# Two-layer transformer kernel: the second scores and the mixing of blocks 2 and 3 made in pairs of head groups, with block 3's queries held aside

## The chip, the core and the metric

The kernel runs on one core of a Trainium2 chip. A core has five engines that run side by side, each through its own stream of instructions, and that wait for one another through semaphores: TensorE (PE in the profile; its weight loads are PEld), VectorE (DVE), ScalarE (ACT), GpSimd (POOL) and SyncE (SP), which here only issues transfers (DMAs). SBUF is the working memory of 128 partitions, PSUM the small memory that PE writes its results to, in eight banks of 128 partitions by 512 float32 values. The metric is the time of one execution on the device in microseconds (us), as the median of several runs.

## The reference

Four layers in a row, each on the normalized input and added to it. The input x is 4 sequences of 512 tokens with 256 features.

```python
x = x + L0_attn(layernorm(x))   # 16 heads of 16, causal, over the 512 tokens of a sequence
x = x + L0_ffn(layernorm(x))    # 8 experts, the best 2 per token AND per output feature
x = x + L1_attn(layernorm(x))   # 16 query heads of 128, 4 key heads; attends over the 4 sequences
x = x + L1_ffn(layernorm(x))    # gated, 2048 inner units, weights unpacked from 4 bits

# L0_attn, the part that the change touches
qkv = einsum('bsd,od->bso', x, w_project)            # q, k, v: [b, 16, 512, 16]
att = einsum('bhqd,bhkd->bhqk', q, k) / sqrt(16)
att = softmax(where(causal, -1e9, att))
out = einsum('bhqk,bhkd->bhqd', att, v)
return einsum('bsd,od->bso', out, w_out)
```

## The kernel before

**Blocks, sequences, head groups.** The 512 positions of a sequence are four blocks j of 128. Layer 0's attention works on the queries of one block j, one sequence s and one or more head groups g (four heads each) at a time, a *batch*. Block 0 takes 4 head groups in a batch, block 1 takes 2, blocks 2 and 3 take 1, so there are 4 + 8 + 16 + 16 = 44 batches, in the order of j, then s, then g. Block j's queries meet the keys of blocks 0 to j: 384 keys for block 2, 512 for block 3. `qk` holds, per head group, four slots with the keys of the four blocks and two more (4 and 5) with queries; block j's queries go to slot 4 + j % 2, so block 2 takes over block 0's slot and block 3 takes over block 1's.

**The softmax in two passes.** The first scores (`greatest`, L631) put the queries on the partitions; `mask` (L644) adds a large negative number to the masked part and DVE takes the maximum of each row (L650, four reductions per batch, one for each head of a group). `shift` (L660, L663) transposes the maxima on PE and subtracts them on DVE from the rows of the queries that are kept for it, so that the second scores come out less the maximum. The second scores (`powers`, L679) put the keys on the partitions: for each chunk c of 128 keys and each head one matmul with 128 query columns. ACT takes the exponent (L688), POOL sets the masked part to 0 (L698). `mixed` (L715) multiplies by the values, which carry a column of ones for the softmax's sum, and ACT copies the result (L723). `divided` transposes it (L733), divides on DVE (L740, L741), transposes again (L750), and after the block's last sequence makes the output product (L762) and adds it to the residual (L772). Then `hidden_pieces` normalizes the block for the feed-forward part.

**Buffers.** PSUM has five banks for scores (`ps_sc`, used in turn by four first and four second scores), one for the transposed maxima and the mixing (`ps_mm`), and two for everything else (`ps_dn`).

**The order of the work.** For PE, DVE and POOL the order is that of the program. It is written out by a loop over the batches n. Step n emits: first scores of batch n+1, shift of n, mask and maxima of n+1; a *fill*; mixing of n-1; second scores of n; another fill. A fill opens a *slot*: it hands out a budget of estimated PE and DVE time, and takes pieces from a list of streams, in the order of the list, as long as budget is left and a piece's conditions hold (`need(engine, cost, gap, cond)`; the gap is the number of slots since the stream's last piece). The streams are the preparation of later blocks (`prepare`, `projections`), the divisions, and the feed-forward part of layer 0: `logit_pieces` and `result_pieces` (L226, the *products*, estimated at 1.85 of PE each; 128 in all, eight for each of 16 groups of 128 tokens, four of a block), `weight_pieces` (the choice of the best two, on DVE) and `addition_pieces`. What is left of the feed-forward part when layer 0's attention is done is spread over layer 1's attention, whose loop over p stands at p = 10 until the last addition.

**Preparation of a block.** `project` makes 128 rows of keys or queries for a block (L529), ACT copies them to `stage` (L533, one buffer), and eight DMAs bring the stage's keys and queries to `qk` (L539, SP's queue). Layer 1's weights for q, k, v (`wqkv`, L916) are loaded into memory that layer 0 leaves.

## Time and profile before

| | |
|---|---|
| median of 3 runs | 1183.99 us (1183.14 to 1185.19) |
| the profiled execution | 1185.96 us, its span 1184.2 us |
| PE busy | 1153.4 us, 97% of the span |
| DVE busy | 807.9 us, 68% |
| ACT busy | 485.2 us, 41% |
| block 2's batches | 138 to 263 us |
| block 3's batches | 263 to 392 us |
| second scores (L679) | 1280 records, 54.1 us |
| mixing (L715) | 1280 records, 46.2 us |
| granted PE clock | 0.995 |

The span runs from the first to the last instruction that the profile shows; the execution's own time has a little around it. Each float32 matmul is two records. Busy times are unions, so records that overlap count once. A line of the timeline has the start, the length, the engine, the line in the kernel, the operation, what it writes and reads, the shape (rows x columns of the array that are used, then the moving operand) and the number of merged records; in brackets the idle time of the engine before it and what ended that. A line of the table by stage has the length of the stretch and each engine's busy time in it with its instructions in parentheses.

### The profile page before, as it was taken

The page shows a single profiled execution, that of the slowest core. Times are in us where ns is not written, and L with a number is a line of the kernel's source. Part 1 is how long each engine was busy: PE and PEld are TensorE (multiplying, and loading weights), DVE is VectorE, ACT ScalarE, POOL GpSimd, SP SyncE. Part 2 cuts the span into 40 slices and gives each one's busy share as a digit, 9 for nine tenths or more (in the row PEclk, how much of TensorE's full clock was granted, in tenths as well). Part 3 has the DMA queues.
Part 4 walks back from the last instruction along what each step waited for, and adds up shares of the span by engine and source line. Part 5 has one row for each costly group of instructions (what it writes and reads, how often), then busy time and mean ns, then how long its engine had stood idle before and what let it go on. Part 6 is the DMA issues. An engine that isn't in the chain of part 4 may idle for free.

```text
span 1184.2 us, 18603 instructions
## 1 busy us (share of the span) xinstructions
PE 1153.4 (97%) x7178; PEld 666.0 (56%) x7178; DVE 807.9 (68%) x1783; ACT 485.2 (41%) x1099; POOL 106.4 (9%) x152
## 2 busy tenths in 40 slices
PE   7999999999999899999999999999999999999998
PEld 3666555555555445555555556566644465475487
DVE  5676779889889777368646783888599844725710
ACT  1434545555466444445344542455244322303300
POOL 7322112112111000000000000000000000000000
PEclk9999999999999999999999999999999999999999
DMA  7230010000000310000000001021010000000000
GB/s 216 66 79 2 16 22 1 2 1 1 2 1 2 117 62 1 1 1 1 1 1 1 1 7 31 18 65 26 18 52 4 0 1 18 0 1 18 1 12 24
DMA packets 21240, 26.46 MB, mean 22 GB/s; under 512 B 5128, under 2 KB 14600, under 8 KB 21152
## 3 DMA queue, kind: packets, MB, share of 16 engines
q1 hardware_dynamic: 20480, 24.10, 7.4%
q10 hardware_dynamic: 672, 1.18, 0.4%
q8 instruction: 56, 0.92, 0.3%
q14 instruction: 32, 0.26, 0.1%
HBM read 18.97 MB, written 2.10 MB: 18 GB/s over the span
## 4 chain that ended last, share of the span: by engine, by line
PE 82%; DVE 11%; ACT 2%; issue 2%; POOL 1%; DMA 1%; SPq 0%; ACTq 0%; DVEq 0%; POOLq 0%
PE qk_ps L967 11%; PE o L1058 10%; PE y L1214 9%; PE g L895 9%; PE u L895 9%; PE lg_ps L226 8%; PE eo L226 8%; PE s L631 4%; PE s L679 3%; DVE mx L650 3%; PE av L715 2%; PE v_ps L949 2%; PE qk_ps L529 2%; PE a L1038 1%; PE s L980 1%
## 5 line engine op out<-in xcount | busy, mean ns | idle before, releaser
L967 PE MATMUL qk_ps<-xT,wqkv 128*128 128x512 f32 x320 | 148.6, 598 | 0.3 <-ACT qT L971 0.3
L226 PE MATMUL lg_ps<-rw,xT 128*128 128x512 f32 x256 | 123.6, 607 | 3.9 <-ACT xT L934 1.6
L226 PE MATMUL eo<-ew,xT 128*128 128x512 f32 x256 | 122.4, 601 | 3.2 <-ACT part L315 1.0
L1058 PE MATMUL o<-wpj,oT 128*128 128x256 f32 x512 | 119.8, 382 | 0.0
L1214 PE MATMUL y<-wd,it 128*128 128x256 f32 x512 | 111.8, 379 | 0.0
L1058 PEld LDWEIGHTS o<-wpj,oT 128*128 128x128 f32 x512 | 95.7, 190 | 27.7 <-issue 15.1
L1214 PEld LDWEIGHTS y<-wd,it 128*128 128x128 f32 x512 | 97.0, 190 | 15.0 <-issue 2.2
L650 DVE TENSOR_REDUCE mx<-s 128x1 f32<-128x384 f32 (+3 forms) x176 | 100.5, 633 | 1.4 <-PE s L644 1.4
L967 PEld LDWEIGHTS qk_ps<-xT,wqkv 128*128 128x128 f32 x320 | 59.4, 190 | 68.7 <-issue 59.6
L688 ACT ACTIVATE pt<-s 128x512 f32<-128x512 f32 (+1 forms) x176 | 83.7, 560 | 23.4 <-PE s L679 23.4
L895 PE MATMUL g<-xT,wgu 128*128 128x512 f32 x192 | 90.4, 593 | 0.0
L895 PE MATMUL u<-xT,wgu 128*128 128x512 f32 x192 | 90.2, 592 | 0.0
L315 ACT ACTIVATE part<-eo,c 128x256 f32<-128x256 f32 x128 | 53.8, 472 | 86.5 <-PE eo L226 85.0
L698 POOL TENSOR_SCALAR_AFFINE_SELECT pt<-pt 128x256 f32<-128x256 f32 (+2 forms) x88 | 60.7, 696 | 266.5 <-ACT pt L688 265.8
L1192 ACT ACTIVATE th<-sq 128x512 f32<-128x512 f32 x64 | 40.3, 630 | 87.8 <-DVE sq L1191 87.8
L226 PEld LDWEIGHTS eo<-ew,xT 128*128 128x128 f32 x256 | 46.4, 191 | 49.0 <-issue 37.4
L226 PEld LDWEIGHTS lg_ps<-rw,xT 128*128 128x128 f32 x256 | 46.3, 191 | 49.2 <-issue 36.8
L214 DVE TENSOR_TENSOR xres<-xres,y 128x256 f32<-128x256 f32 x16 | 6.7, 421 | 92.2 <-PE y L1214 92.2
L177 POOL TENSOR_TENSOR ln_rs<-rs_v,minus_half 128x4 f32<-128x4 f32 x16 | 18.0, 1124 | 553.2 <-DVE rs_v L176 455.6
L631 PE MATMUL s<-qk 32*128 32x128 f32 (+3 forms) x512 | 62.2, 465 | 1.2 <-ACT pt L688 0.9
L1193 DVE SCALAR_TENSOR_TENSOR th<-th,g 128x512 f32<-128x512 f32 x63 | 43.2, 686 | 29.2 <-ACT th L1192 29.2
L289 ACT COPY lg<-lg_ps 128x512 f32<-128x512 f32 x64 | 37.6, 587 | 62.1 <-PE lg_ps L226 61.9
(233 smaller groups left out, 1763.2 us busy)
## 6 DMA issues: line engine op xcount, KB each, us to landing
qk<-stage SPq DMA_DIRECT2D x56, 64.0 KB, 2.4
wqkv<-in_w_qkv SPq DMA_DIRECT2D x8, 320.0 KB, 7.4
rw<-in_router_w SPq DMA_DIRECT2D x8, 256.0 KB, 7.5
ew<-in_expert_w SPq DMA_DIRECT2D x8, 256.0 KB, 4.6
wpj<-in_w_proj SPq DMA_DIRECT2D x1, 2048.0 KB
out<-xres SPq DMA_DIRECT2D x4, 512.0 KB, 2.6
xres<-in_x SPq DMA_DIRECT2D x3, 512.0 KB, 9.1
dq_wgu<-in_gate_w SPq DMA_DIRECT2D x8, 128.0 KB, 2.4
```

The costliest lines, as they stand in the source:

```text
L226: nc.tensor.matmul(ps, lhsT=xT[:, hc, (g % 4) * P : (g % 4 + 1) * P], rhs=w[:, hc, 2 * pair : 2 * pair + 2, :].rearrange("p e o -> p (e o) ...
L315: nc.scalar.mul(part[:, e % 4], ps[:, i], c[:, e : e + 1])
L631: nc.tensor.matmul(tiles[h][:, b * nk : (b + 1) * nk].rearrange("p (c k) -> p c k", k=P), lhsT=queries(j, g)[r, s], rhs=qk[r, g, : j + 1, ...
L650: nc.vector.tensor_reduce(maxes[n % 2][:, h, gs[0] : gs[0] + nb], ps[:, : nb * nk].rearrange("p (b k) -> p b k", b=nb), AX.X, ALU.max,)
L688: nc.scalar.activation(pt[:, i, : nb * nk], tiles[2 * pair + i][:, : nb * nk], AF.Exp, scale=0.25)
L698: nc.gpsimd.affine_select(out=last, in_=last, compare_op=ALU.is_ge, fill=0.0, base=0, pattern=pattern, channel_multiplier=-1,)
L895: nc.tensor.matmul(ps, lhsT=wgu[:, w, half, jj, par * P : (par + 1) * P], rhs=xT[:, half, :], start=half == 0, stop=half == 1,)
L967: nc.tensor.matmul(ps, lhsT=wqkv[:, hc, kv, h, :], rhs=xT[:, hc, :], start=hc == 0, stop=hc == 1,)
L1058: nc.tensor.matmul(ys[t // 2][:, t % 2], lhsT=state["o"][:, h, t * P : (t + 1) * P], rhs=wpj[:, HPK * kv + h, :], start=kv == 0 and h == 0 ...
L1192: nc.scalar.activation(th, sq, AF.Tanh, scale=0.7978845608028654)
L1193: nc.vector.scalar_tensor_tensor(th, th, 1.0, gp, ALU.add, ALU.mult)
L1214: nc.tensor.matmul(ps, lhsT=it[:, c // 2, c % 2, t * P : (t + 1) * P], rhs=wd[:, c // 2, c % 2, :], start=c == 0, stop=c == 2 * NJ - 1,)
```

## The change

Batches 0 to 11 (blocks 0 and 1) stay. From batch 12 on, the batches of blocks 2 and 3 alternate: for each s and g first block 2's, then block 3's. The first scores, masks, maxima and shifts are still made per batch. The second scores and the mixing are made per *pair*:

- `pair_powers(m, 0)` takes the keys of blocks 0 and 1 against the queries of blocks 2 and 3 together (256 columns in a matmul); `pair_powers(m, 1)` takes the keys of block 3 (against block 3's queries alone) and of block 2 (against both). The second half's exponents go to a buffer `lasts`, in the memory of the projection weights `wp`, which are not needed by then; one select on POOL per two heads masks both blocks' last chunks.
- `pair_mixed(m)` adds up all four key blocks for both blocks' queries in one group of matmuls, and ACT copies the two halves.
- The loop has one step more (45). Even steps from 14 on emit `pair_powers(m, 1)` with no mixing before it, odd steps from 15 on emit `pair_mixed(m - 1)` and `pair_powers(m, 0)`.
- Block 3 has to be prepared before step 12. Its preparation starts at step 5 in place of 7. Its queries go to a stage of their own for both halves and are placed into slot 5 in two parts, s = 0, 1 after 8 batches and s = 2, 3 after 12, when block 1 no longer needs them (`place_queries`, 16 DMAs each); its keys go straight to their slot (16 DMAs).
- Blocks 2 and 3 are divided one after the other for each s (`both_divided`), and their output products, now a stream of its own (`output_0`), both come after the last pair. The normalization for layer 1's first block is made from step 40 on.
- The fills of block 3's steps get PE budgets of 1.8 and 2.2 in place of 1.6 and 2.0.

```diff
+            if j == 3:
+                nc.scalar.copy(stage[:, half] if i else stage, ps)
+                if not i:
+                    for r in range(8):
+                        h = 32 * (r % 4)
+                        nc.sync.dma_start(out=qk[h + 4 : h + 20, 2 * half + r // 4, j]...,
+                            in_=stage[16 * r : 16 * r + 16])
+                return
...
+        def place_queries(stage, s):
+            for r in range(16):
+                h, half = 32 * (r % 4), r // 8
+                nc.sync.dma_start(
+                    out=qk[h + 4 : h + 20, r // 4, 5, s : s + 2].rearrange("p s q -> p (s q)"),
+                    in_=stage[16 * (r % 8) : 16 * (r % 8) + 16, half, s * P : (s + 2) * P],
+                )
...
+            if j == 3:
+                qs = a1.tile([P, 2, 512], F32, tag="stage", name="stage3")
+                for half in range(2):
+                    yield need("PE", 1.75, 2)
+                    project(j, xT, half, qs, 1)
+                for half in range(2):
+                    yield need("PE", 1.75, 1, cond=lambda: blanked >= 10)
+                    ks = a1.tile([P, 512], F32, tag="keys", name=f"keys3_{half}")
+                    project(j, xT, half, ks, 0)
+                for s in (0, 2):
+                    yield need("PE", 0.0, 0, cond=lambda: done >= 8 + 2 * s)
+                    place_queries(qs, s)
+                return
...
+        FIRST = 12
+        batches[FIRST:] = [
+            (j, s, range(g, g + 1)) for s in range(NS) for g in range(4) for j in (2, 3)
+        ]
...
+        def pair_powers(m, second):
+            _, s, gs = batches[FIRST + 2 * m]
+            g = gs[0]
+            tiles = [ps_sc.tile([P, 512], F32, tag="sc", name=f"p{m}_{second}_{h}") for h in range(4)]
+            to = 0
+            for c in (3, 2) if second else (0, 1):
+                q = qk[:, g, 5 if c == 3 else 4 : 6, s, :]
+                at, to = to, to + q.shape[1] * P
+                for h in range(4):
+                    r = slice(32 * h, 32 * h + 32)
+                    nc.tensor.matmul(
+                        tiles[h][:, at:to].rearrange("p (c k) -> p c k", k=P),
+                        lhsT=qk[r, g, c, s, :], rhs=q[r], start=True, stop=True,
+                    )
...
+        def pair_mixed(m):
...
+            for c in range(4):
+                of, nq = (0, 256, P, 0)[c], 1 if c == 3 else 2
+                for r in range(4):
+                    at = c * per_block + (s * NH0 + 4 * g + r) * 17
+                    pt = powers_of[m, c // 2][r // 2][:, r % 2, of : of + nq * P]
+                    nc.tensor.matmul(
+                        av[32 * r : 32 * r + 32, 2 - nq : 2], lhsT=va[:, at : at + 32],
+                        rhs=pt.rearrange("p (b k) -> p b k", k=P), start=c == 0, stop=c == 3,
+                    )
...
-        for n in range(NBT):
+        for n in range(NBT + 1):
...
-            if n in (1, 7):
+            if n in (1, 5):
...
+            if n == NBT - 4:
+                streams.insert(
+                    0, Stream(norm_pieces(0, b1, b2, normed_first, cond=lambda: (3, 1) in added))
+                )
...
-                if n:
+                if 0 < n <= FIRST:
                     mixed(n - 1)
-                powers(n)
+                elif n > FIRST + 1 and not second:
+                    pair_mixed(m - 1)
+                if n < FIRST:
+                    powers(n)
+                elif n > FIRST:
+                    pair_powers(m, second)
...
-        mixed(NBT - 1)
-        streams.insert(0, Stream(norm_pieces(0, b1, b2, normed_first)))
-        last = Stream(divided(*batches[NBT - 1][:2]))
-        streams.insert(0, last)
-        while last.next is not None:
+        behind_powers = False
+        fill(PE=2.0, DVE=2.6)
+        pair_mixed(15)
+        streams.insert(0, Stream(both_divided(NS - 1)))
+        while not {4 * j + t for j in (2, 3) for t in (0, 2)} <= resolved or not normed_first:
             fill(PE=2.0, DVE=2.6)
```

## The prediction, made before the changed kernel ran

> **What bounds the kernel now.** I read the page's busy shares first, then the chain that ended last, then the table by stage for the two stretches in which blocks 2 and 3 run (138 to 263 us and 263 to 392 us, read off the transposes of the maxima at L660).
>
> ```profile
> span 1184.2 us, 18603 instructions
> PE 1153.4 (97%) x7178; PEld 666.0 (56%) x7178; DVE 807.9 (68%) x1783; ACT 485.2 (41%) x1099; POOL 106.4 (9%) x152
> ...
> PE 82%; DVE 11%; ACT 2%; issue 2%; POOL 1%; DMA 1%; SPq 0%; ACTq 0%; DVEq 0%; POOLq 0%
> ```
> ```profile
> 138.00:263.00 125.00, 120.77 (x1145) 64.58 (x1146) 102.99 (x265) 66.30 (x194) 22.06 (x34) 0.96 0.06 10
> 263.00:392.00 129.00, 125.33 (x1398) 68.92 (x1396) 112.54 (x261) 71.65 (x185) 22.05 (x33) 1.00 0.01 2
> ```
>
> The first number after the stretch is its length, then PE, PE's loads, DVE, ACT and POOL. PE is the bound everywhere, but here DVE is busy 82% and 87% of the time, so it is the second bound, and PE's busy time contains waits: a group of matmuls that stops half way is still shown as busy. So I measure each group of matmuls by its shortest form and call the rest a wait.
>
> **Second scores, the heart of the change: worth nothing.** Per pair of batches the old code issues 3 + 4 chunks of four matmuls with 128 columns (56 records, two to a matmul, in two groups). The new one issues two chunks of 256 columns, then one of 128 and one of 256: 32 records. The columns that stream are 7 x 128 = 896 in both. What is a column worth in wide and in narrow matmuls? The first scores show it, with 512 columns for four heads in three widths:
>
> ```profile
> 39.39 1.17 PE L631 MATMUL s<-qk 32*128 32x128 f32 x32
> ...
> 58.78 1.15 PE L631 MATMUL s<-qk 32*128 32x256 f32 x16
> ...
> 310.78 1.14 PE L631 MATMUL s<-qk 32*128 32x512 f32 x8
> ```
>
> 1.17, 1.15 and 1.14 us: halving the instructions gives 0.02 us. The Trainium skill speaks for the change here ("TensorE: Matmul & The Clock Gate", LDWEIGHTS): a weight load lasts its columns divided by 1.2 in ns, however few rows it has, and by its section on packing small matmuls it overlaps a running matmul only in another row group. Per row group the pair drops from 7 to 4 loads of two records, so the rule would give up to 3 x 2 x 107 ns = 0.64 us a pair, 10 us over 16 pairs. This trace's loads last 187 ns (L679), longer than the rule's, and are hidden all the same. I take the row: 16 x 0.02 = 0.3 us, called 0. Bounds: 0 to -10.
>
> **Mixing: -2.2 us.** From start to the next group's start the mixing of block 2 (24 records) takes 0.79 us at its shortest, of block 3 (32 records) 1.01: 0.22 for each chunk of 128 columns and 0.13 once per group. One group of 896 columns: 7 x 0.22 + 0.13 = 1.67 against 1.80, so 0.13 to 0.14 a pair, 16 pairs: -2.2. With one group instead of two, the wait for the only buffer of the `mm` pool (av behind L663's subtraction, 0.16 in the batch shown next) also comes half as often: waits at L715 sum to about 3 us in these stretches, a third of it saved, -1. The ACT exponents keep their columns; POOL's selects go from four to two of double width, hidden (POOL is busy 17%).
>
> **The moved cover: +6 us.** The second scores use five PSUM buffers together with the first scores of the next batch, so their fourth head waits until DVE has read the third maximum of that next batch (L650). PE issues in order: the projection, product or first score behind such a matmul waits with it, and ACT's exponents after it. Two batches show what hides this:
>
> ```profile
> 188.09 0.39 PE L644 MATMUL s<-later,ident_h 128*128 128x128 bf16 x4
> 188.41 1.98 PE L226 MATMUL eo<-ew,xT 128*128 128x512 f32 x4
> 188.49 1.95 DVE L650 TENSOR_REDUCE mx<-s 128x1 f32<-128x384 f32 x4
> 190.33 0.86 PE L715 MATMUL av<-pt,va 128*32 128x128 f32 x24
> 191.12 0.95 PE L679 MATMUL s<-qk 32*128 32x128 f32 x24
> ...
> 337.12 0.39 PE L644 MATMUL s<-later,ident_h 128*128 128x128 bf16 x4
> 337.53 2.48 DVE L650 TENSOR_REDUCE mx<-s 128x1 f32<-128x512 f32 x4
> 337.67 1.08 PE L715 MATMUL av<-pt,va 128*32 128x128 f32 x32 [0.16 <-DVE qk L663]
> 338.68 1.94 PE L679 MATMUL s<-qk 32*128 32x128 f32 x32
> ```
>
> In the first, a product of the feed-forward part (1.9 us) and the mixing (0.8) lie between mask and second scores, which run in 0.95. In the second the planner had no product, the mixing alone was the cover, and they took 1.94 instead of 1.17: 0.77 us lost. After the change the mixing stands ahead of every other second-score group only: in the steps that mask block 2's batch (odd n) the cover grows to 1.67, in those that mask block 3's (even n), whose maxima are the longer ones, it is gone. From the first mask matmul, the third maximum of a block 3 batch ends after 2.29 us when DVE is on time and up to 3.60 when it is late. With one product and no mixing the second scores start at 2.09 us, and their fourth head is due 0.11 later. Taking the mixing's 1.01 us out of the 16 block 3 batches: six with a product and DVE on time lose at most 0.09 each; six with DVE late lose 0.25, 0.59, 1.17, 0.94, 1.40 and 0; four with less than a product lose 1.86, 1.63, 1.64, 1.64. Sum 11.6, against 3.3 by the same rule today: +8.3. The odd steps save block 2's 2.3 us of such waits nearly whole: -2. Net +6. Bounds: 0 (DVE, which gains time while PE waits, is never late) to +12 (products run short more often).
>
> **Block 3's projection: -3 us.** It now runs before step 12, and its queries are copied into one buffer for both halves instead of a `stage` buffer that must be emptied by eight DMAs between the halves. Today:
>
> ```profile
> 153.30 1.11 ACT L533 COPY stage<-qk_ps 128x512 f32<-128x512 f32 x2
> 153.97 1.99 PE L762 MATMUL o<-wo,aT 128*128 128x256 f32 x8 [2.25 <-ACT stage L533]
> ```
>
> Late copies leave no PSUM buffer and PE waits; with 1.03 and 0.62 us at the projections of 138 and 148 us that is 3.9 us. I take -3, since the second half of the keys still waits for eight DMAs (2.4 us to landing, a fill slot of about 4 us between them); bounds -4 to 0. Placing costs 48 DMAs where there were 16. They stand in SP's queue, where nothing follows until the next layer's weights at 402 us; the second placing waits for the last batch of block 1 and is needed only when block 3's s = 2 starts, some 16 steps later. Cost 0; without that cover one landing, 2.4 us.
>
> **The end of the layer: +4.5 us.** Today block 2 is finished at 289 us and its tokens feed the products from 309 us on; four products of token group 8 run between 380 and 411 us. Now blocks 2 and 3 finish together, so until then only 64 products (groups 0 to 7) exist; some 60 had run by the same point today. Behind the end stand twice as many divisions and output products (4.6 us of PE work, moved and not added), two or three fill slots more, and one step more in the loop (45 for 44). Then the weights of layer 1 wait, as today, for the last output product:
>
> ```profile
> 400.35 1.99 PE L762 MATMUL o<-wo,aT 128*128 128x256 f32 x8 [0.93 <-ACT part L315]
> 402.38 6.01 SPq L916 DMA_DIRECT2D wqkv<-in_w_qkv  x10
> 408.97 1.07 ACT L934 COPY xT<-xT_ps 128x512 f32<-128x512 f32 x2 [0.18 <-DMA wqkv<-in_w_qkv]
> ```
>
> From 400.35 to the value products at 411.43 PE has 11.1 us, filled with three products of 1.81, one output product of 2.0 and 1.2 of transposes: 2.5 idle. With none or one of the three left, and one product less to wait behind, the idle part is 4.3 to 6.1: +2 to +3.5, say +2.7. For one or two missing products in the last steps, at the 0.8 that such a step loses, and the longer tail +1.8. The products themselves are not lost, layer 1 spreads what is left. Block 3's tokens still wait for group 7. Bounds 0 to +15, the upper end if the products come so late that layer 1's step 10, which waits for the last addition (740.5 us today, just in time), has to stand still.
>
> **The sum.** 0 - 2.2 - 1 + 6 - 3 + 4.5 = +4.3 us. The profiled execution took 1185.96 us (its span 1184.2 and 1.8 around it), so 1190.3 in its terms; it stands 1.97 above the median of the runs, 1183.99. Predicted: 1188.3 us.
>
> **Rivals.** (a) As summed, +2.4 to +12: 0.44. (b) DVE is not late and the cover isn't missed: the +6 becomes 0 and the end costs 2, which gives -4.2, 1180; for it speaks that the batches with a product and DVE on time lose only 0.09. It decides from the point where the third maximum is read within 2.2 us of the mask. Against it speaks DVE's 87%. 0.22. (c) The weight loads do limit the second scores: -10 and the rest as summed, 1178; the three widths speak against it: 0.05. (d) It ends within 2.4 us, gains and losses cancel, 1184: 0.17. (e) The late tokens hold layer 1 at its step 10: +15 in place of +4.5, 1199; against it, the planner shares what is left over nine steps: 0.12.
>
> **How the numbers follow.** 0.2%, 2.4 us, is about what a measurement of this kernel can tell from no change. Faster is (b) and (c), 0.27; same is (d), 0.17; slower is (a) and (e), 0.56. The likeliest case, (a), alone spans 1186.4 to 1196. The range takes in (b), (d), (a) and most of (e): 1178 to 1202.
>
> **What would show it.** Right: about 16 groups of second scores a layer with their span near 1.15 and 16 near 0.94 when they don't wait; mixing groups of some 1.7 us, 16 of them; second scores after a product alone that are stretched by DVE's maxima, hardly any after the mixing; no wait on the stage copy; fewer products between the last output product and the value products. Wrong: unstretched second scores of 896 columns a pair that take well under 1.9 us, even steps without stretch, or product supply that lasts through the end.

## The result

The changed kernel takes 1224.01 us, the median of four runs (1221.63 to 1227.1), against 1184.06 us before in the same session: a ratio of 1.0337, 95% interval 1.032 to 1.0353. It is 40 us slower. The prediction was 1188.3 us with a range of 1178 to 1202; the sign was right, the size off by a factor of about nine.

The page of the changed kernel: the span, the busy times, the granted PE clock in 40 slices (before it was 9 in every slice), and the shares of the chain that ended last.

```profile
span 1223.6 us, 16999 instructions
...
PE 1177.6 (96%) x6410; PEld 666.3 (54%) x6410; DVE 813.4 (66%) x1783; ACT 482.8 (39%) x1099; POOL 93.7 (8%) x120
...
PEclk9999889999889898999999999999999999999999
...
PE 78%; DVE 16%; ACT 2%; issue 1%; POOL 1%; DMA 1%; SPq 0%; DVEq 0%; ACTq 0%; POOLq 0%
```

PE has 24 us more of busy time although it executes 768 records fewer, and its share of the chain fell from 82% to 78% while DVE's rose from 11% to 16%. The clock row is new: it has dips in slices 5 to 16 (122 to 490 us). The mean granted clock is 0.978 where it was 0.995.

Where the time went is read from the table by stage, with stretches that begin and end at the same instruction in both kernels (steps at the transposes of the maxima, L660 before and L700 after; layer 1's groups at the transposes of their scores on DVE). First before: step 11; steps 12 to 42; from step 43 to the first scores of layer 1; the first group of layer 1.

```profile
128.82:137.88 9.06, 9.06 (x91) 4.83 (x88) 7.85 (x15) 4.61 (x10) 0.98 (x3) 1.00 0.01 2
137.88:380.51 242.63, 235.41 (x2428) 127.92 (x2427) 207.19 (x508) 131.33 (x362) 41.63 (x63) 0.98 0.03 6
380.51:438.62 58.11, 50.93 (x252) 24.47 (x249) 44.00 (x124) 29.78 (x81) 4.98 (x6) 1.00 0.28 91
438.62:466.82 28.20, 27.67 (x137) 13.99 (x138) 21.70 (x46) 12.52 (x25) 1.01 (x1) 1.00 0.00 1
```

The same four stretches after; the columns are the length, then PE, PE's loads, DVE, ACT and POOL with instructions in parentheses, then the granted clock, the DMA share and GB/s.

```profile
126.94:143.95 17.01, 14.27 (x100) 7.15 (x96) 12.16 (x18) 5.38 (x11) 1.89 (x2) 0.92 0.14 34
143.95:403.10 259.15, 245.82 (x1631) 118.95 (x1630) 216.34 (x513) 129.16 (x359) 29.30 (x32) 0.93 0.01 2
403.10:465.20 62.10, 56.25 (x275) 30.17 (x274) 28.18 (x84) 26.11 (x65) 3.29 (x4) 0.97 0.26 85
465.20:504.05 38.85, 32.20 (x139) 16.80 (x140) 30.29 (x76) 13.52 (x36) 1.77 (x1) 0.87 0.00 0
```

Four places are longer: step 11 by 7.9 us (clock 0.92), steps 12 to 42 by 16.5 (clock 0.93), the end of the layer by 4.0, the first group of layer 1 by 10.7 (clock 0.87). Steps 4 to 10 are 1.9 us shorter, the rest of layer 1 is 2.0 longer. The experiments, described below, are read by the same stretches. Each has its ratio to the kernel before in its own session, whose median lay between 1184.06 and 1185.56 us, so single differences to 1224.01 can be off by some 1.5 us.

| us | before | after | e2 | e7 | e8 | e10 | e11 | e4 | e6 |
|---|---|---|---|---|---|---|---|---|---|
| steps 4 to 10 | 60.4 | 58.5 | 59.0 | 58.4 | 58.6 | 58.8 | 58.4 | 60.3 | 60.7 |
| step 11 | 9.1 | 17.0 | 17.6 | 17.5 | 11.5 | 17.4 | 11.5 | 9.1 | 9.1 |
| steps 12 to 42 | 242.6 | 259.2 | 238.9 | 239.4 | 257.8 | 261.9 | 239.6 | 240.2 | 240.5 |
| step 43 to layer 1's first scores | 58.1 | 62.1 | 62.0 | 64.2 | 62.1 | 62.1 | 62.0 | 61.7 | 56.3 |
| layer 1, first group | 28.2 | 38.9 | 38.5 | 39.1 | 38.8 | 18.8 | 18.8 | 31.9 | 28.2 |
| groups 2 to 9 | 216.5 | 216.8 | 216.8 | 216.8 | 216.9 | 225.8 | 225.8 | 220.5 | 216.5 |
| groups 10 to 16 | 149.4 | 151.0 | 151.0 | 151.0 | 151.0 | 152.5 | 152.6 | 152.6 | 149.4 |
| time at half clock, before the kernel's end | 10.2 | 54.6 | 23.9 | 37.5 | 47.8 | 54.6 | 13.7 | 17.1 | 6.8 |

The last row is the sum of the stretches in which the trace's clock record shows 0.5; each is 3.41 us or a multiple of it. A PE that streams all the time loses half of such a stretch, so the 44 us more after the change can hold at most 22 of the 40 us.

Two steps of the changed kernel in a row, step 35, in which the second scores run freely (odd: block 2's mask at 335.12), and step 36 (even: block 3's mask at 344.35), in the timeline.

```profile
335.12 0.39 PE L684 MATMUL s<-later,ident_h 128*128 128x128 bf16 x4
...
335.34 1.94 PE L227 MATMUL eo<-ew,xT 128*128 128x512 f32 x4
...
337.20 1.07 PE L788 MATMUL av<-pt,va 128*32 128x256 f32 x16
...
338.09 0.83 PE L788 MATMUL av<-lasts,va 128*32 128x256 f32 x16
...
338.86 1.15 PE L755 MATMUL p<-qk 32*128 32x256 f32 x16
...
341.12 0.42 ACT L407 ACTIVATE spare<-owing 128x256 bf16<-128x256 f32 x1 [1.37 <-DVE owing L417]
...
341.53 2.04 ACT L766 ACTIVATE pt<-p 128x512 f32<-128x512 f32 x4
341.85 2.41 PE L671 MATMUL s<-qk 32*128 32x512 f32 x8
...
344.35 0.39 PE L684 MATMUL s<-later,ident_h 128*128 128x128 bf16 x4
...
344.67 0.48 PE L755 MATMUL p<-qk 32*128 32x128 f32 x2
344.76 2.47 DVE L690 TENSOR_REDUCE mx<-s 128x1 f32<-128x512 f32 x4
...
345.49 2.84 PE L755 MATMUL p<-qk 32*128 32x128 f32 x14 [0.34 <-DVE mx L690]
...
348.26 3.78 PE L227 MATMUL lg_ps<-rw,xT 128*128 128x512 f32 x4
```

In the first step a product (1.94) and the pair's mixing (1.07 + 0.83) lie between mask and second scores, which run in 1.15 us. Their exponents (L766) begin only at 341.53: ACT works in order, and ahead of them it has an operation of the feed-forward part (L407) that waits 1.37 us for DVE. So block 3's first scores (L671), which need the buffers that the exponents free, take 2.41 us where 1.14 is enough. In the second step there is neither a product nor a mixing. The second scores begin 0.3 us after the mask, stop after two records for a score buffer that DVE's maxima (344.76, 2.47 us long) still hold, and the whole group takes from 344.67 to 348.26, 3.6 us, where 0.9 is enough. Then the product behind it takes 3.78 us in place of the usual 1.9: the clock fell to 0.5 from 346.1 us on.

Summed over the stretch, each group from its start to the start of the next, the differences to before are (us):

| group | before | after | difference |
|---|---|---|---|
| products (49 of 1.89, 52 of 2.06) | 92.8 | 107.1 | +14.4 |
| block 3's first scores (16 of 1.41, 15 of 2.20) | 22.5 | 33.1 | +10.6 |
| second scores | 39.3 | 46.2 | +6.8 |
| masks, with the wait behind them | 9.4 | 13.8 | +4.4 |
| block 2's first scores (14 of 1.29, 15 of 1.02) | 18.1 | 15.3 | -2.8 |
| mixing | 28.9 | 26.5 | -2.4 |
| block 3's projection | 7.0 | 0 | -7.0 |
| output products | 7.6 | 3.8 | -3.9 |
| other groups | 17.1 | 13.4 | -3.6 |
| steps 12 to 42 | 242.6 | 259.2 | +16.5 |

Of the products' 14.4 us, 5.7 are three products more, and 8.8 their longer time, nearly all of it in stretches at half clock. The second scores of even steps take 1.90 us in the mean against 0.87 when nothing holds them, those of odd steps 1.18 against 1.08; that is 17 us of stretch where the kernel before had 8.7, of which 2.3 were the stage wait behind one group. So the stretch rose by some 10 us. Most of it, 13 us, lies in six even steps (30, 32, 34, 36, 38 and 42) whose first fill has no product.

Block 3's first scores do not stand behind those stretched groups. They stand in the odd steps, behind second scores that run nearly freely, and wait for their exponents. In steps 15, 25, 27 and 41 no product lies between the two, and they take 6.3, 2.9, 3.7 and 3.0 us. In steps 15, 17, 27, 31, 35 and 39 the exponents begin 2.0 to 4.0 us after the start of the second scores, with a feed-forward operation directly ahead of them on ACT, where six other odd steps have 1.2.

### The profile page after: what moved, and what is told of

Read it like the earlier page. It is cut to its first block, busy times and chain, and to the rows that moved or that the text cites. A ratio compares the mean times of both kernels' runs of the same rounds, so it can differ in the third digit from the quotient of the medians.

```text
span 1223.6 us, 16999 instructions
## 1 busy us (share of the span) xinstructions
PE 1177.6 (96%) x6410; PEld 666.3 (54%) x6410; DVE 813.4 (66%) x1783; ACT 482.8 (39%) x1099; POOL 93.7 (8%) x120
## 3 DMA queue, kind: packets, MB, share of 16 engines
q10 hardware_dynamic: 672, 1.18, 0.4%
## 4 chain that ended last, share of the span: by engine, by line
PE 78%; DVE 16%; ACT 2%; issue 1%; POOL 1%; DMA 1%; SPq 0%; DVEq 0%; ACTq 0%; POOLq 0%
PE qk_ps L1088 10%; PE y L1335 9%; PE o L1179 9%; PE g L1016 8%; PE u L1016 8%; PE lg_ps L227 8%; PE eo L227 7%; PE s L671 4%; DVE mx L690 3%; PE p L755 2%; PE v_ps L1070 2%; PE qk_ps L531 2%; PE av L788 1%; PE a L1159 1%; PE s L1101 1%
## 5 line engine op out<-in xcount | busy, mean ns | idle before, releaser
L227 PE MATMUL lg_ps<-rw,xT 128*128 128x512 f32 x256 | 131.0, 638 | 1.0 <-ACT xT L1055 0.7
L227 PE MATMUL eo<-ew,xT 128*128 128x512 f32 x256 | 124.9, 612 | 2.1 <-ACT part L316 0.8
L1179 PEld LDWEIGHTS o<-wpj,oT 128*128 128x128 f32 x512 | 95.8, 190 | 28.2 <-issue 15.6
L227 PEld LDWEIGHTS lg_ps<-rw,xT 128*128 128x128 f32 x256 | 49.3, 202 | 52.4 <-issue 46.1
L671 PE MATMUL s<-qk 32*128 32x128 f32 (+3 forms) x512 | 67.5, 481 | 6.3 <-ACT pt L766 3.5
L1016 PEld LDWEIGHTS u<-xT,wgu 128*128 128x128 f32 x192 | 36.5, 190 | 45.9 <-issue 44.5
L1016 PEld LDWEIGHTS g<-xT,wgu 128*128 128x128 f32 x192 | 36.2, 190 | 45.1 <-issue 41.3
```

The costliest lines, as they stand in the source:

```text
L227: nc.tensor.matmul(ps, lhsT=xT[:, hc, (g % 4) * P : (g % 4 + 1) * P], rhs=w[:, hc, 2 * pair : 2 * pair + 2, :].rearrange("p e o -> p (e o) ...
L671: nc.tensor.matmul(tiles[h][:, b * nk : (b + 1) * nk].rearrange("p (c k) -> p c k", k=P), lhsT=queries(j, g)[r, s], rhs=qk[r, g, : j + 1, ...
L1016: nc.tensor.matmul(ps, lhsT=wgu[:, w, half, jj, par * P : (par + 1) * P], rhs=xT[:, half, :], start=half == 0, stop=half == 1,)
L1179: nc.tensor.matmul(ys[t // 2][:, t % 2], lhsT=state["o"][:, h, t * P : (t + 1) * P], rhs=wpj[:, HPK * kv + h, :], start=kv == 0 and h == 0 ...
```

## The experiments

The steps of the prediction that could have failed so badly were the cover moved out of the even steps, the placing, and the late tokens. The first theory was the missing cover; its rivals were the order of the batches itself, SP's queue, the late tokens, and later the vector engine's work and the clock. The larger PE budgets in block 3's steps stay in every run made from the changed kernel; they were not tested alone.

**e1: the order and the placing alone.** The batches alternate as in the change, block 3 is prepared in the same way and the tokens come late, but second scores and mixing are per batch, as before.

```diff
-                elif n > FIRST + 1 and not second:
-                    pair_mixed(m - 1)
-                elif n > FIRST:
-                    pair_powers(m, second)
+                if n:
+                    mixed(n - 1)
+                powers(n)
```

> The changed kernel with the second scores and the mixing made per batch again, 128 columns at a time, a mixing in every step; what stays of the change is the alternating order, the early preparation of block 3 with its queries held aside, and the late finish of blocks 2 and 3. Theory A, the pairing itself costs the time, since every even step has lost its mixing as a cover and PE's clock drops after such waits: some 16 us of the stretch of blocks 2 and 3 come back, about 1206 us, granted clock above 0.99. Theory B, order and late tokens cost the time: no less than 1218 us.

1217.48 us, ratio 1.0278 (1.0259 to 1.0296). Most of the loss is there without any pair of second scores: step 11 is 17.0 us, the first group of layer 1 39.1, and steps 12 to 42 still take 256.3. Here the mixing stands in every step, so that the stretch is exposed in another way, in the timeline:

```profile
350.51 1.17 PE L719 MATMUL s<-qk 32*128 32x128 f32 x32
351.50 1.02 PE L671 MATMUL s<-qk 32*128 32x512 f32 x2
354.06 2.81 PE L671 MATMUL s<-qk 32*128 32x512 f32 x6 [1.54 <-ACT pt L728]
```

Here a step's second fill has no product, the first scores (L671) come directly behind the second scores and wait for the buffers that ACT's exponents (L728) still read; then the clock falls (0.5 from 355.3 us on). So neither the pair form nor a missing mixing is needed for a loss in this stretch. Why e1's stretch is 17 us longer than that of e2, which has the same order, is known in part: block 3's first scores take 2.37 us in e1 and 1.72 in e2, 9.8 us in all. In step 15 they take 5.8 against 2.7. There ACT has a feed-forward operation (L383), which waits 1.90 us for DVE, ahead of the exponents in e1, as in the changed kernel (2.25 us), and behind them in e2 and e7. The rest is open.

**e2: pairs of second scores, mixing in both steps.** The changed kernel, with each block's mixing in a step of its own.

```diff
-                elif n > FIRST + 1 and not second:
-                    pair_mixed(m - 1)
+                elif n > FIRST + 2:
+                    block_mixed(m - 1, second)
```

> The changed kernel with its wide second scores, but the mixing split by query block: block 2's in the odd steps, block 3's in the even ones, ahead of the second half's scores (the fourth buffer for exponents is the stage that is free by then). Theory A, the missing cover: the groups of second scores with 128 and 256 columns come down from a mean of 1.94 us to about 1.2, the granted clock rises above 0.99, about 1206 us. Theory B: within 4 us of the changed kernel's 1224.

1207.19 us, ratio 1.0192 (1.016 to 1.0223): 17 us are back by the medians, 19.4 by the spans, all of it in steps 12 to 42, which fall to 238.9, below the 242.6 of before. The second scores of even steps fall from 1.90 to 1.20 us in the mean, block 3's first scores from 2.20 to 1.72, and the half-clock time from 54.6 to 23.9 us.

**e3: block 3's keys on ACT's queue.** SP's queue held all 32 placing transfers ahead of the keys' 16, though the program emits the keys' first: its order is not that of the program. In the timeline of the changed kernel:

```profile
117.26 20.65 SPq L592 DMA_DIRECT2D qk<-stage  x32
...
133.81 1.88 PE L531 MATMUL qk_ps<-xT,wp 128*128 128x512 f32 x4
...
138.02 8.29 SPq L540 DMA_DIRECT2D qk<-keys  x10
...
140.07 3.94 PE L671 MATMUL s<-qk 32*128 32x512 f32 x8 [2.67 <-DMA qk<-keys]
```

The last key product is done at 135.7; the keys' transfers start at 138.02, when SP has issued the last placing (20.65 us for 32, 0.65 each), and the first scores of block 3 wait 2.67 us for the first of them and then run in pieces, 3.94 us for 1.14. The edit gives the keys another queue.

```diff
-                        nc.sync.dma_start(
+                        nc.scalar.dma_start(
                             out=qk[h + 4 : h + 20, 2 * half + r // 4, j].rearrange(
```

> The changed kernel with the 16 transfers of block 3's keys issued from ACT's queue instead of SP's, where they stand behind all 32 placing transfers, the last 16 of which wait for block 1's last batch. Theory: step 11 to 12 takes 17.0 us in the changed kernel against 9.1 before, 6 of them for the keys; they come back, about 1218 us, and the wait of PE for the keys (2.7 us at 137 us) is gone. Rival, the placing itself or the drain costs it: within 2 us of 1224.

1223.51 us, ratio 1.0325 (1.031 to 1.0341): nothing gained. The wait went over to ACT, as the timeline shows:

```profile
135.56 5.51 ACTq L540 DMA_DIRECT2D qk<-keys  x8
...
141.81 3.78 PE L227 MATMUL lg_ps<-rw,xT 128*128 128x512 f32 x4 [5.67 <-ACT lg L290]
```

Eight transfers hold ACT for 5.51 us, 0.69 each, and PE waits 5.67 us for the copy behind them. So this run didn't tell the theories apart; e8 does.

**e4: the kernel before with late tokens.** Block 2's tokens are handed to the feed-forward part only with block 3's.

```diff
+            if j == 2:
+                return
+            if j == 3:
+                streams.insert(fold_at, Stream(hidden_pieces(2)))
+                fold_at += 1
             streams.insert(fold_at if j else 0, Stream(hidden_pieces(j)))
```

> The kernel before, with one thing of the change: block 2's tokens are handed to the feed-forward part only when block 3's are, at the end of layer 0's attention. If the late tokens cost what the end of layer 0 and the first head group of layer 1 lost in the changed kernel (4 and 10.6 us), about 1198 us; if the planner makes up for them in layer 1, within 3 us of 1184, as I had predicted no more than 2 for them.

1197.53 us, ratio 1.0108 (1.0091 to 1.0125), 12 us slower than before (1185.56 in that session) by this one edit. The end of the layer takes 3.6 us more, the first group of layer 1 3.7, groups 2 to 9 4.0 and groups 10 to 16 3.2; steps 12 to 42 get 2.4 shorter. The prediction had looked for the price at the end of the layer only and set 4.5.

**e5: the changed kernel, with idle matmuls in the empty even fills.** Two matmuls that write to a spare buffer stand where an even step's first fill had given PE nothing.

```diff
+            if n > FIRST and second and left["PE"] == given:
+                ps = ps_dn.tile([P, 512], F32, tag="dn", name=f"warm_{n}")
+                for i in range(2):
+                    nc.tensor.matmul(ps, lhsT=ident, rhs=wo..., start=not i, stop=i == 1)
```

> The changed kernel with two extra matmuls of 512 columns (1.8 us, result not used) in those even steps whose first fill gave PE nothing, so that PE works while it would wait for DVE's maxima of 2.5 us; nothing is left out. If half of the loss in blocks 2 and 3 is the clock that drops after such waits (54 us at half speed in the changed kernel, 11 before), the granted clock rises towards 0.99 and the time falls by 5 to 10 us, to about 1216, although work is added. If the waits alone cost the time, or the clock drops for other reasons: 1224 to 1230, clock 0.978.

1222.26 us, ratio 1.0319 (1.0304 to 1.0335). The stretches at half clock between 223 and 359 us are gone and steps 28 to 35 are 4.3 us shorter. In steps 32, 34 and 36, where the idle matmuls stand, 1.87 us of them ahead of the second scores bring these from 3.6, 2.9 and 3.6 us to 1.1, the product behind them in steps 32 and 36 from 3.7 to 1.9, and the steps from 9.1, 9.5 and 9.1 to 6.1, 7.8 and 6.1. So an empty place costs the wait and then the clock: filled with work of no use, such a step is up to 3 us shorter. The whole gains little of this, 1.8 us by the medians: the half-clock time is still 44.4 us, 13.7 of it now between 386 and 421 us.

**e6: the kernel before, with the mixing of two batches together.** From step 16 on the mixing of two batches follows in every even step, and the odd steps have none. Neither order, placing nor tokens change.

```diff
-                if n:
+                if 0 < n < 15:
                     mixed(n - 1)
+                elif n > 15 and n % 2 == 0:
+                    two_mixed(n - 2)
```

> The kernel before, in its own order and with its own scores, with only the mixing moved: from step 16 on the mixings of two batches stand together in every second step, and none in the others. Theory, the moved cover costs the time by itself: slower by 8 to 20 us, 1193 to 1205, with second scores stretched in the steps without mixing. Rival, the moved cover costs only where tokens run short at the end: within 4 us of 1184.

1181.32 us, ratio 0.9968 (0.9959 to 0.9976): faster than both kernels. The theory that taking the mixing out of every second step costs 8 to 20 us by itself is refuted. Steps 12 to 42 take 240.5 us, 2.1 less than before.

The odd steps here had a product ahead of their second scores in nearly all cases. Three did not (19, 33 and 37), and their second scores took 2.2, 2.8 and 2.8 us; behind that of step 33 the clock was at 0.5 for 6.8 us, the only such stretch of the run. The odd steps from 15 on with a product take 1.3 in the mean, where 0.9 (block 2) and 1.1 (block 3) are enough. So taking a mixing out of a step costs little when a product stands there, and between one and two us and sometimes the clock when none does.

**e7: the changed kernel, with the pair's mixing in even steps.** The same instructions, the same number of them; the mixing moves by one step, from the odd to the even ones. It needs the exponents' buffer one step longer, so every fourth goes to another memory.

```diff
-                elif n > FIRST + 1 and not second:
+                elif n > FIRST + 2 and second:
                     pair_mixed(m - 1)
```

> The changed kernel with the whole pair's mixing in the even steps, ahead of the second half's scores (behind block 3's longer maxima), and none in the odd ones. Theory, each step needs its cover and the longer maxima need it more: between the split mixing (1207) and the changed kernel (1224), about 1212, with the wide first-half scores (256 columns) now stretched. Rival, only the even steps matter: 1207 or less.

1208.88 us, ratio 1.0207 (1.0188 to 1.0226), between the two expectations. Steps 12 to 42 fall from 259.2 to 239.4. The timeline of an even step without a product, as the one at 344.35 above:

```profile
332.85 0.39 PE L684 MATMUL s<-later,ident_h 128*128 128x128 bf16 x4
333.40 1.07 PE L789 MATMUL av<-pt,va 128*32 128x256 f32 x16 [0.16 <-DVE qk L703]
334.29 0.83 PE L789 MATMUL av<-lasts,va 128*32 128x256 f32 x16
335.05 1.06 PE L755 MATMUL p<-qk 32*128 32x128 f32 x16
336.04 1.98 PE L227 MATMUL lg_ps<-rw,xT 128*128 128x512 f32 x4
```

The mixing alone covers: the second scores take 1.06 us and the product behind them 1.98. Their mean over the even steps is 0.93, where it was 1.90; the odd steps' rises from 1.18 to 1.77 and no further, since those have products in most cases and the shorter maxima. This is the cleanest of the runs: 20 us hang on which of the two steps the mixing stands in. The second scores themselves give only 5.7 of them (-14.6 in the even steps, +8.9 in the odd ones). Block 3's first scores give 7.9, the products, with less half clock, 5.1, and the wait behind the masks 3.4; the other groups together take 2.4 more.

**e8: the keys before the queries.** Block 3's key products come first in the preparation, then the query products.

```diff
-                for half in range(2):
-                    yield need("PE", 1.75, 2)
-                    project(j, xT, half, qs, 1)
                 for half in range(2):
-                    yield need("PE", 1.75, 1, cond=lambda: blanked >= 10)
+                    yield need("PE", 1.75, 2, cond=lambda: blanked >= 10)
                     ks = a1.tile([P, 512], F32, tag="keys", name=f"keys3_{half}")
                     project(j, xT, half, ks, 0)
+                for half in range(2):
+                    yield need("PE", 1.75, 1)
+                    project(j, xT, half, qs, 1)
```

> The changed kernel with block 3's keys projected before its queries, so that the 16 key transfers stand ahead of the 32 placing transfers in SP's queue. Moving them to ACT's queue gained nothing, because ACT itself was held for 5.5 us by eight issues of about 0.66 us. Theory, it is the issue time of 48 transfers just before step 12: with the keys issued some four steps earlier, 5 to 8 us come back, about 1217. Rival, the drain before step 12 costs it whatever the order: 1222 to 1226.

1217.8 us, ratio 1.0279 (1.0262 to 1.0297). The timeline at the same place:

```profile
116.61 13.15 SPq L540 DMA_DIRECT2D qk<-keys  x16
...
132.22 9.84 SPq L592 DMA_DIRECT2D qk<-stage  x13
...
136.65 1.14 PE L671 MATMUL s<-qk 32*128 32x512 f32 x8
```

The keys' sixteen transfers now stand ahead of the placing, and block 3's first scores take 1.14 us without a wait. Step 11 falls from 17.0 to 11.5 us, the whole by 6. Of the 7.9 us that step 11 had lost, 2.4 remain.

**e9: one product a fill.** A fill of layer 0 emits one product at most from step 13 on. In the changed kernel some fills have two products and the first fills of even steps 32, 34 and 36 none; in this run each of these three has one.

```diff
+            if (engine, cost) == ("PE", 1.85) and made_now >= most:
+                return False
```

> The changed kernel, in which a fill of layer 0 may emit one product at most from step 13 on (the feed-forward streams' budgets are otherwise kept), so that the second of two products that stood together in an odd step's last fill moves into the next even step's first fill, which was empty: steps 28, 32, 34 and 36 get a product between the mask's matmuls and block 3's second scores. Theory A (the even first fills were empty because products fall two at a time, and the empty fill exposes the maxima, about 2 us each time, and then the clock): steps 28 to 36 fall from 71.4 us towards the 62.7 of the kernel with the mixing in both steps, fewer stretches at half clock, the whole 1210 to 1217. Theory B (products are short because the vector engine makes weights too slowly, and one moved product only opens a hole elsewhere): 1221 to 1226, and the stretches at half clock come in other steps.

1220.6 us, ratio 1.0306 (1.0284 to 1.0327): between the two expectations. Steps 32, 34 and 36 fall from 9.1, 9.5 and 9.1 us to 6.1, 7.0 and 7.6, and steps 12 to 42 from 259.2 to 252.1, in the direction of the first theory; but the odd steps 27, 29, 31 and 35 get 7.5 us longer in all, the end of the layer takes 2.0 more, and the half-clock time stays at 54.6 us, 20 of it now between 380 and 425 us (there the changed kernel has 10). What these steps gain others lose, as the second theory said.

**e10: less for DVE at the start of layer 1.** The waits of the changed kernel that are longest in all, apart from that at its start (engine, tile, line and what it waited for; total us, times, the longest), and then the timeline of its first group in layer 1:

```profile
PE av L788 <- DVE qk L703: 6.6, 5, 2.4
PE s L671 <- ACT pt L766: 3.5, 3, 2.3
PE xT_ps L203 <- DVE junk L414: 3.4, 1, 3.4
...
PE qk_ps L1088 <- ACT qT L1092: 2.9, 2, 2.6
PE s L671 <- DMA qk<-keys: 2.7, 1, 2.7
```

```profile
479.71 3.41 PE L1088 MATMUL qk_ps<-xT,wqkv 128*128 128x512 f32 x4 [2.58 <-ACT qT L1092]
486.51 1.97 PE L203 MATMUL xT_ps<-ident,xn 128*128 128x128 f32 x8 [3.40 <-DVE junk L414]
489.16 3.78 PE L227 MATMUL lg_ps<-rw,xT 128*128 128x512 f32 x4 [0.68 <-ACT xT L1055]
```

The waits on `qT` and `junk` are this group's. PE stands because DVE has a run of feed-forward work to do in order (the tokens of blocks 2 and 3 were resolved together at the end of layer 0), and ACT, in order too, waits for results of that run ahead of the copies that the attention needs. Then the clock halves (3.78 us for a product). The edit takes DVE's allowance in this group from about 2.4 to 1.2.

```diff
-            fill(PE=1.9 * share + 0.2, DVE=dve or 2.7 * share + 1.4)
+            fill(PE=1.9 * share + 0.2, DVE=dve or 2.7 * share + 1.4 if p > 0 else 1.2)
```

> The changed kernel, with the vector engine's allowance per gap in layer 1's first group (p = -1 and 0) at 1.2 in place of 2.7 x share + 1.4 (about 2.4). Theory A (the first group of layer 1 takes 38.8 us against 28.2 because the tokens of blocks 2 and 3, resolved together at the end of layer 0, let loose feed-forward work that the vector engine does in order ahead of the attention's own, so that the scalar engine and the PE wait behind it): that group falls by 5 to 10 us, the whole 1214 to 1219. Theory B (it is long for another reason, such as the weights of the group coming late or fewer products standing in it): that group stays within 2 us, the whole 1222 to 1227.

1219.35 us (1213.57 to 1219.4), ratio 1.0283 (1.0255 to 1.0312). The timeline of that place:

```profile
475.29 5.42 PE L1088 MATMUL qk_ps<-xT,wqkv 128*128 128x512 f32 x12
480.86 1.65 PE L203 MATMUL xT_ps<-ident,xn 128*128 128x128 f32 x8
482.34 1.89 PE L1179 MATMUL o<-wpj,oT 128*128 128x256 f32 x8
```

The group falls from 38.9 to 18.8 us, with no wait and the full clock. Three of its products (5.6 us) moved to later groups, and groups 2 to 9 take 9.0 us more. From step 43 to the end the kernel is 9.0 us shorter (1217.6 - 406.1 against 1223.6 - 403.1); layer 0, whose edit it was not, happened to take 3.0 longer in this execution, with eleven half-clock stretches before step 43 in place of eight. The group's excess is thus the burst, and about half of it comes back as work done later.

**e11: three of the edits at once.** The changed kernel with e2's mixing, e8's keys and e10's allowance. Pairs of second scores, order and late tokens stay.

```diff
+                    block_mixed(m - 1, second)
...
+                    yield need("PE", 1.75, 2, cond=lambda: blanked >= 10)
                     ks = a1.tile([P, 512], F32, tag="keys", name=f"keys3_{half}")
...
+            fill(PE=1.9 * share + 0.2, DVE=dve or 2.7 * share + 1.4 if p > 0 else 1.2)
```

> The changed kernel with three of the earlier edits at once: the mixing per block in both steps of a pair, block 3's keys ahead of its queries, and the vector engine's allowance at 1.2 in layer 1's first group; the wide second scores, the order in pairs and the late tokens remain. Theory A (the loss is made of separate parts: the mixing in one step, the queue at step 11, the burst at the start of layer 1, and the late tokens, which remain): the three gains add, 1224.0 - 16.8 - 6.2 - 4.7 = 1196.3, so 1193 to 1200, about what the kernel before with block 2's tokens held back takes (1197.5). Theory B (the parts are one wait that moves about, and what one edit gains another already has): 1202 to 1208, hardly under the 1207.2 of the split mixing alone.

1189.36 us, ratio 1.0054 (1.0033 to 1.0075): 34.7 us are back, where the single gains add to 16.8 + 6.2 + 4.7 = 27.7 by the medians. By the ratios it is some 33.5 against 30.5, which the intervals do not tell apart; the gains add at least. The same four stretches:

```profile
127.50:138.96 11.46, 11.39 (x99) 5.88 (x96) 10.85 (x17) 4.88 (x11) 1.89 (x2) 1.00 0.13 30
138.96:378.59 239.63, 232.49 (x1969) 119.17 (x1966) 214.98 (x512) 130.84 (x361) 30.21 (x32) 0.98 0.01 3
378.59:440.62 62.03, 54.82 (x323) 29.93 (x322) 29.69 (x87) 26.44 (x65) 3.29 (x4) 0.97 0.26 85
440.62:459.46 18.84, 18.16 (x109) 9.21 (x110) 14.96 (x34) 7.79 (x16) 1.01 (x1) 1.00 0.01 1
```

Step 11 is at 11.5 us, steps 12 to 42 at 239.6, 3.0 below before, the first group at 18.8, and the clock is whole but for 0.98 and 0.97 in the second and third stretch. 34.7 of the 40 us come back with three placements, none of which adds or removes arithmetic. What is left, 5.6 us between the two spans, is 3.9 at the end of the layer and 3.2 in groups 10 to 16, where e4 has 3.6 and 3.2 too, and 1.5 in the sum of the others, against the 3.0 gained in steps 12 to 42.

**e12: e6 with one product a fill.** The rule of e9 from step 17 on, which gives steps 19 and 37 of e6 a product.

```diff
+            most = 1 if n > 16 else 9
```

> The kernel before with the mixing of two batches together from step 16 on, and with one product at most per fill from step 17 on, which puts a product into steps 19 and 37, the odd steps that had neither mixing nor a product ahead of their second scores (step 41 loses its own). Theory A (each uncovered step costs about 2 us): 1176 to 1180, a little faster than the 1181.3 of the pairing alone. Theory B (the pace is set by the vector engine's weights, one product more here is one less there): 1180 to 1184.

1182.65 us (1180.19 to 1185.71), ratio 0.9982 (0.9974 to 0.9991): no better than e6. The second theory holds: what one step gains, another lacks. e6 remains the fastest kernel.

## Why the prediction was wrong

**Second scores, 0: right.** The pair's groups take 1.15 and 0.94 us where nothing holds them, as forecast, against 0.95 and 1.17 before, so 56 records made into 32 give nothing (2.09 us a pair for 2.12). Of the up to 10 us that the rule on weight loads would have given nothing shows.

**Mixing, -2.2: right in size.** A pair's mixing takes from 337.20 to 338.86, 1.66 us for a forecast of 1.67. In e6, with two batches' mixing in one group, the mixing takes 25.9 us of the stretch for 28.9 before, 3.0 less, where the prediction's two terms of this kind make 3.2. The -1 for the wait at the mixing buffer had the wrong sign: the mixing waited 1.0 us in all for DVE's shift before, and 6.6 after (the first line of the waits shown).

**The moved cover, +6: this is the step that failed most.** Its own term was too small, but inside its bounds of 0 to +12: the stretch of the second scores rose by some 10 us. It was made up otherwise than forecast. The prediction gave 4.9 us to twelve even steps with a product ahead, nearly all of it for DVE being late; there were nine, and they lost 2.4. It gave 6.8 to four steps with less than a product; there were six without one, and they lost 13. For the rest the prediction took the products from where they lay in the profile of before, step by step; in the new order they lie elsewhere, and even steps 32, 34 and 36, in which nothing else stands either, got none. e6 shows that the same removal costs little where a product stands. The term was thus a matter of which steps the planner leaves empty, and the old trace could not tell that.

What failed beyond its size is the sentence "PE issues in order: the projection, product or first score behind such a matmul waits with it, and ACT's exponents after it": it was written down and not priced. The products grew by 8.8 us at half clock, some 6 of them directly behind stretched even groups (310.7, 328.8, 348.3 and 398.5 us). Block 3's first scores, +10.6 us, had no term of any kind: they wait in the odd steps, whose second scores were hardly held, for exponents that come late on ACT. The wait between mask and mixing adds 4.4 more. Much of this depends on the place of the mixing: put back ahead of the even steps' second scores, alone or in both steps, it gives 20 us of the stretch back (e7, e2). How much of that is the cover and how much the order that ACT gets with it was not separated; in step 15 alone ACT's order differs and the step takes 11.2 us against 7.1.

**The clock: no term at all.** The mean of 0.995 in the profile before stood for three stretches of 3.4 us, and the sum took it as given. The changed kernel has eleven with 54.6 us. No run sets the clock by itself, so that the share of it (at most 22 us) isn't separated from the waits that come with it; where the waits were taken away, it recovered (e2, e7, e11), and in two steps of e5, where idle matmuls filled the wait, the product behind was back at 1.9 us.

**Block 3's projection, -3 and placing, 0.** The stage waits went, as forecast, and steps 4 to 10 are 1.9 us shorter, although two of block 3's four projections now stand in them. Placing failed: "they stand in SP's queue, where nothing follows until the next layer's weights" is untrue, since the keys of the same block follow. At 0.65 us an issue, 32 of them are 21 us of queue. Step 11 got 7.9 us longer, of which e8 gives 5.5 back. The bound set for it, one landing of 2.4 us, counted the transfer and not the issue.

**The end of the layer, +4.5: right in size by luck, wrong as a whole.** That stretch got 4.0 us longer, but not for the reason given. The prediction expected the products to run short between the last output product and layer 1's value products. There the changed kernel takes 8.6 us with two products and 0.5 of wait (428.05 to 436.61), where it was 11.1 with three products and 2.5 of wait, and 4.3 to 6.1 of wait were forecast. Ahead of that PE waits for the divisions of the last two blocks, 1.86 and 1.14 us, and half of the output products run in part at half clock, 5.30 us for 3.62. The rest came behind it: the burst in the first group of layer 1, +10.7, and +2.0 after, had no term. Held tokens alone cost 12 us (e4). Of the prediction's bound of +15, the mechanism was the wrong one: layer 1 did not stand still at its step 10.

**The sum.** Of the rivals, none came near. The one with late tokens, 1199, had the largest price and the wrong place. With the three faults in the placement mended (e11) the change costs 5.6 us in the spans, next to the +4.3 of the sum. That is no confirmation of it, since e11 has neither the moved cover nor the pair's mixing that the sum had priced. What the sum lacked was what the moved pieces collide with: 16.5 us in steps 12 to 42, where its terms made -0.2 (+6 - 2.2 - 1 - 3), 7.9 at the placing for 0, and 12.7 in layer 1 for 0.

## What to carry to other kernels

When PE's order is fixed, an instruction that is moved takes its cover with it, so for each place that it leaves list what remains between the wait's start and the next user, and price the whole row behind it and not the waiting group alone. Look at the order of the other engines too: here ACT did feed-forward work ahead of the exponents that PE needed. Which places a planner leaves empty can't be read off the old trace: count products in each fill of the new order before relying on them. A small transfer costs its queue an issue each time, and the queue's order decides, so see what stands behind a batch of them, on whichever engine issues.

## What the hardware showed that I had not expected

The PE clock fell to 0.5 without a long idle stretch. Between 137 and 403 us of the changed kernel the longest wait that the profile shows for PE is 2.7 us, and still eight stretches of 3.4 or 6.8 us at half clock lie there; ahead of the one at 346.1 us there were only a first-score group of 2.41 us and a second-score group that was held up. The Trainium skill ("TensorE: Matmul & The Clock Gate", HAM oscillation) gives gaps above about 3.4 us as what to avoid. That rule alone foresees none of these stretches, and the measurement decides: groups with holes in them were enough here. A product in such a stretch takes 3.78 us for 1.88, so a wait of 2 us can cost 4.

The same order of PE's work in layer 0 gave stretches in other places from one execution to another: e10 and the changed kernel have the same PE instructions up to step 43 and reach it at 406.1 and 403.1 us, with eleven and eight such stretches by then.

A transfer of 16 partitions held its issuing queue 0.65 us on SP and 0.69 on ACT, where it also stopped ACT's arithmetic; and SP's queue was not in the order in which the program emits.
